# Inverses and scores as 64x64 tiles, and one plain key for two heads, in a gated delta-rule kernel

## The chip, the cores and the metric

One core of one Trainium2 chip runs the whole program. The metric is device time in microseconds (us) of one execution; the median of three runs stands for the kernel. Engines: PE (TensorE) multiplies matrices, PEld is its weight load, DVE (VectorE), ACT (ScalarE) and POOL (GpSimd) work on vectors, SP (SyncE) issues the DMAs. Each engine takes its instructions in the order in which the program lists them.

## The reference, cut to what matters

The input is 4 sequences of 1024 rows of 256 numbers. The attention has 16 key heads and 32 value heads of size 128 (two value heads share a key head), and works in chunks of 64 rows. For one value head and one chunk, with `k`, `q` normalized, `beta` the gate of the row, `gc` the running sum of the log decay:

```python
decay = exp(gc[i] - gc[j]) on and below the diagonal
A  = -(k_beta @ k.T * decay) * strictly_lower
Tm = inverse(eye - A)                         # 64 x 64: the "inverse"
u   = Tm @ v_beta
kcd = Tm @ (k_beta * exp(gc))
attn  = (q @ k.T) * decay                     # 64 x 64: the "scores"
v_new = u - kcd @ S                           # S: the state, 128 x 128
out   = (q * exp(gc)) @ S + attn @ v_new
S     = S * exp(gc[-1]) + (k * exp(gc[-1] - gc)).T @ v_new
```

The chunks of a sequence follow each other through `S`; sequences and heads do not depend on each other. The result is normalized, multiplied by `silu(z)` and projected; layer norms, residuals and a gated feed-forward layer follow, whose weights are looked up in a table of 16 numbers. All of it is in float32.

## The kernel before

The 32 value heads are handled in 8 groups of 4 (`HG`), with 2 key heads (`MG`) each. A step (`step`) handles one chunk of two sequences, `ab` = 0 and 1, for the 4 heads of a group: partitions 0 to 63 hold the 64 rows of one sequence, 64 to 127 those of the other. There are 256 steps. Eight steps make a `Super` (`SB`), of which there are 32. Two steps that follow each other belong to the two pairs of sequences, so that a state is used in every other step.

A step goes through six stages, separated by `yield`, and works as follows (lines are those of the profile):

- `pv`, `x0`: the values are transposed (L680) and scaled (L684).
- `pkqs`: key and query times state, two products in two banks (L693), one after the other. DVE adds the first to `x0` (L704, four instructions), ACT scales the second into `qs` (L705).
- `px`: inverse times `x0`, four matmuls of a full 128x128 array (L713), one a head. The weights `ue` hold the inverses of the two sequences as blocks on the diagonal, and zeros elsewhere. ACT copies `px` into `xs` (L718), negated.
- `pk`, `kt`: the keys are transposed (L722), and ACT makes four scaled copies, one for each head, by the factor `cd` of the row (L726). POOL decays the state (L730).
- `po`: scores times `xs`, four full matmuls (L713) with block-diagonal weights `ae`; DVE adds `qs` and makes `core` (L737). ACT squares `core` (L742).
- `pu`: key times `xs`, eight matmuls over 64 rows (L749); DVE adds the result to the state (L758).

`channel` makes the columns of q, k and v in advance (matmuls `pp` L432, a convolution over 4 rows: one ACT instruction L446 and three DVE instructions L449, silu L453). `norms` and `scores` make the squares, the factors `cc` (L505) and `cd` (L511) and the scores; `invert` finds 32x32 inverses on DVE (`rank` L589, `v` L590), and `build` completes them to 64x64 on PE (`m1`, `m2`). `expand` fetches the weights `ue`, `ae` and the chunk's key and query `qku` from DRAM for the step after. `project_out` makes `pz` (L143), transposes (`pto` L800) and projects (`pout` L807), and DVE adds the result to `ac` (L810 and L812).

The order is written out by hand: `SLOTS` gives one line for each of the eight steps of a super, in which each letter advances one generator by one stage. `N0`, `N1`, `N2` are the first three stages of the step, `O3`, `J`, `O4` the last three of the step before. A typical slot on PE is `pp` (A), `po` (O3), `pv` (N0), `pto` (T), `pu` (O4), `pkqs` twice (N1), `pz` (Z), `pp` (B), `px` and `pk` (N2), `pout` (U), with `kkq`, `pn` or `m1`, `m2` between in some slots.

All PSUM banks but those of `pp`, `pu` and `pgu` come from one pool of four (`bank`), handed out in turn: a bank is free once the readers of the bank that was handed out four allocations earlier are done. The doubles `pp` and `pu` come from a second pool of two.

Of the kernel before, what the change touches and what calls it, by code (L numbers as in the profile page):

```python
# [64 lines left out]
def delta_net_ffn_kernel(  # L65
# [128 lines left out]
    with tc.tile_pool(name="pre", bufs=2) as pre, tc.tile_pool(name="gates", bufs=1) as gp:  # L194
# [70 lines left out]
        for gs in range(0, NG, 4):  # L265
# [9 lines left out]
            for ab in range(2):  # L275
                ps = bank("pgate")
                T_.matmul(ps, lhsT=sel[ab], rhs=cols, start=True, stop=True)
                el = to[:, :, 4 * GW :].rearrange("p g (t a h) -> p a g t h", a=2, h=HG)[:, ab]
                A.activation(el, ps.rearrange("p (g t h) -> p g t h", g=4, h=HG), AF.Exp)
# [38 lines left out]
    with ExitStack() as main:  # L318
# [16 lines left out]
        zeroed = {}  # L335
        for name in ("ue", "ae"):
            zeroed[name] = [w1.tile(h4, F32, tag=f"{name}{i}", name=name) for i in range(NZ)]
            for t in zeroed[name]:
                G_.memset(t, 0.0)
# [5 lines left out]
        states = [w1.tile([P, 2, HG, P], F32, tag=f"S{p}", name="S") for p in range(NPAIR)]  # L345
# [4 lines left out]
        def load_qk(g):  # L350
# [9 lines left out]
            views.append(dk[:, 4 * nth :].rearrange("p (t a h) -> p t a h", a=2, h=HG))  # L360
# [38 lines left out]
        def channel(k, blk, n, far):  # L399

            last = k.last and blk == 1
            if n < 2 * MG:
                m, j = divmod(n, 2)
                if n == 0:
                    k.qk[blk] = [
                        w1.tile([P, 2, NPAIR, 2, 2, C], F32, tag=f"qk{i}", name=f"qk{i}", bufs=2)
                        for i in range(MG)
                    ]
                    if blk == 0:
                        k.qkd = sd.tile([SB, P, MG, 2, 2 * C], F32, tag="qkd", name="qkd")  # L410
                    if k.g not in w_qk:
                        load_qk(k.g)
                wt = w_qk[k.g][:, :, MG * j + m, :]
                ch = (NK if j else 0) + MG * k.g + m
                dst = k.qk[blk][m][:, :, :, 1 - j, :, :]
# [38 lines left out]
            if n < 2 * MG:  # L454
                nc.sync.dma_start(
                    k.qkd[4 * blk : 4 * blk + 4, :, m, 1 - j, :].rearrange("u p t -> p u t"),
                    dst.rearrange("p n q a t -> p (n q) (a t)"),
                )

        def norms(k, blk):  # L460

            if blk == 0:
                k.n2 = w2.tile([P, SB, MG, 2], F32, tag="n2", name="n2", bufs=5)
                k.cc = w2.tile([P, SB, HG], F32, tag="cc", name="cc", bufs=5)
                k.cd = w2.tile([P, SB, HG], F32, tag="cd", name="cd", bufs=5)
# [8 lines left out]
            for m in range(MG):  # L474
                for j in range(2):
                    src = k.qk[blk][m][:, :, :, j, :, :].rearrange("p n q a t -> p (n q) (a t)")
# [17 lines left out]
            for i in range(4):  # L494
# [16 lines left out]
            V.scalar_tensor_tensor(  # L511
                k.cd[:, us], k.cc[:, us], 1.0, dks[k.g][1][:, t0 : t0 + 4, :], ALU.mult, ALU.mult
            )

# [7 lines left out]
        def scores(k, blk):  # L522
# [24 lines left out]
            for n, (u0, dc) in enumerate(zip(us, dcs)):  # L547
# [3 lines left out]
                for p in range(2):  # L551
                    for m in range(MG):
                        src = k.qk[blk][m][:, n, p]
# [92 lines left out]
        def expand(k, u):  # L646

            at = (supers.index(k) * SB + u) % NZ
            ue, ae = (zeroed[name][at] for name in ("ue", "ae"))
            for q in range(4):  # L650
                rows = slice(q * BS, (q + 1) * BS)
                src = k.vd[q * BS + u * HG : q * BS + (u + 1) * HG, :, :]
                nc.sync.dma_start(ue[rows, :, rows], src.rearrange("h c i -> c h i"))
            for ab in range(2):
                a0 = ab * C
                lo, hi = slice(a0, a0 + BS), slice(a0 + BS, a0 + C)
                hb, w = divmod(u * HG, NQ)
                q = slice((2 * ab + hb) * BS, (2 * ab + hb + 1) * BS)
                nc.sync.dma_start(ue[lo, :, hi], k.nd[q, w : w + HG, :])
                half = slice(a0, a0 + C)  # L660
                nc.sync.dma_start(ae[half, :, half], k.atd[half, u, :, :])
            k.exp[u] = ue, ae
            qku = sc.tile([P, MG, 2, 2, C], F32, tag="qku", name="qku", bufs=2)
            nc.sync.dma_start(qku.rearrange("p m j a t -> p m j (a t)"), k.qkd[u])
            k.qku[u] = qku

        def step(k, u):
# [18 lines left out]
            if not first:  # L686
                got = []
                for j in range(2):
                    ps = bank("pkqs")
                    for m in range(MG):  # L690
                        two = slice(2 * m, 2 * m + 2)
                        for ab in range(2):
                            T_.matmul(  # L693
                                as4(ps)[ab * C : (ab + 1) * C, two, :],
                                lhsT=qk[:, m, j, ab, :],
                                rhs=S_[:, ab, two, :],
# [13 lines left out]
            def applied(w, src, name):  # L710
                ps = bank(name)
                for h in range(HG):
                    T_.matmul(as4(ps)[:, h, :], lhsT=w[:, h, :], rhs=src[:, h, :], start=True, stop=True)  # L713
                return ps

            px = applied(ue, x0, "px")
            xs = t4("xs")
            A.activation(xs, as4(px), AF.Copy, scale=-1.0)  # L718
            if not last:
                pk = bank("pk")  # L720
                for m in range(MG):
                    T_.transpose(as4(pk)[:, m, :], qk[:, m, 0].rearrange("p a t -> p (a t)"), ident)  # L722

                kt = t4("kt")
                for h in range(HG):
                    A.activation(kt[:, h, :], as4(pk)[:, h // 2, :], AF.Copy, scale=k.cd[:, u, h : h + 1])  # L726
                if not first:
                    flat = S_.rearrange("p a h d -> p (a h) d")
                    decay = el[:, ti].rearrange("p a h -> p (a h)").unsqueeze(2)
                    G_.tensor_tensor(flat, flat, bc(decay, [P, 2 * HG, P]), ALU.mult)  # L730
            yield
            po = applied(ae, xs, "po")
            core = t4("core", OUT_LAG)
            if first:
                V.tensor_copy(core, as4(po))
            else:
                V.tensor_tensor(core, as4(po), qs, ALU.add)  # L737
# [6 lines left out]
            if not last:  # L744
                pu = two_banks("pu")
                for h in range(HG):
                    for ab in range(2):
                        half = slice(ab * C, (ab + 1) * C)
                        T_.matmul(  # L749
                            as4(pu[:, ab])[:, h, :], lhsT=kt[half, h, :], rhs=xs[half, h, :], start=True, stop=True  # L750
# [418 lines left out]
```

## Time and profile before

| | |
|---|---|
| median of 3 runs | 4308.6 us (4305.1 to 4310.99) |
| span of the profiled execution | 4307.5 us; no other time of that execution is listed |
| busy PE / PEld / DVE / ACT / POOL | 3986.6 / 2899.0 / 3568.0 / 2831.6 / 2084.0 us |
| instructions | 83434 |
| steps of the delta rule | from about 250 to 3990 us of the span |
| DMA queue | 1052720 packets, 487.64 MB, 42.8% of 16 engines' span |
| granted TensorE clock | 0.984 in the mean, 1.00 from 1000 to 4000 us |

"Busy" is the time in which at least one instruction of the engine ran. A float32 matmul leaves two records, so `x2048` at L713 are 1024 matmuls. "Mean ns" of a matmul holds the time that its results take to come out, which overlaps with the next matmul; what a matmul costs is read from where the next one starts. A line `X <- Y` says that X sat idle until Y ended.

### The profile page before, as it was taken

To read this page: it belongs to the slowest core of one execution; us is meant where nothing else is said; L and a number is where in the kernel's file an instruction comes from. 1 tells how busy PE (TensorE), PEld (TensorE's weight loads), DVE (VectorE), ACT (ScalarE), POOL (GpSimd) and SP (SyncE) were. 2 spreads that over 40 slices of the span, in tenths; PEclk is the share of its full clock that TensorE was granted. 3 is DMA by queue.
4 is the path that set the end of the run, shared out by engine and by line. 5 is a ranking of instruction groups with operands and counts; after the bars stand their busy time and mean duration, and the time that the engine had idled before them with its cause. 6 is when DMAs were issued, how large, how long until landed. Compare 5 with 4: busy or idle time off the path is not lost.

```text
span 4307.5 us, 83434 instructions
## 1 busy us (share of the span) xinstructions
PE 3986.6 (93%) x28544; PEld 2899.0 (67%) x28544; DVE 3568.0 (83%) x6387; ACT 2831.6 (66%) x7279; POOL 2084.0 (48%) x1782
## 2 busy tenths in 40 slices
PE   3679999999999999999999999999999999999999
PEld 2457777777777777767777767777677777767454
DVE  4788888888999888888889998888888998886243
ACT  2467777776777767777677777777777777766211
POOL 2545555555555554555455554555454343434122
PEclk7899999999999999999999999999999999999999
DMA  3444444444444454544454445544454444543011
GB/s 94 120 112 113 116 121 116 123 122 119 128 131 116 114 135 129 134 115 115 129 137 122 109 116 138 135 120 114 121 139 124 119 115 124 137 108 102 26 41 28
DMA packets 1053140, 492.97 MB, mean 114 GB/s; under 512 B 730528, under 2 KB 951856, under 8 KB 1052720
## 3 DMA queue, kind: packets, MB, share of 16 engines
q1 hardware_dynamic: 1052720, 487.64, 42.8%
q8 instruction: 231, 3.78, 0.4%
q14 instruction: 189, 1.55, 0.1%
HBM read 267.66 MB, written 219.69 MB: 113 GB/s over the span
## 4 chain that ended last, share of the span: by engine, by line
PE 49%; DVE 36%; ACT 6%; issue 6%; DMA 2%; SPq 1%; POOL 0%; DVEq 0%; POOLq 0%; ACTq 0%
DVE cv L449 12%; PE pp L432 11%; DVE rank L589 7%; PE pkqs L693 6%; PE pz L143 6%; PE pout L807 5%; PE pgu L970 4%; PE po L713 3%; DVE v L590 3%; PE px L713 3%; DVE core L737 2%; PE pu L749 2%; PE kkq L555 2%; PE py L986 2%; DVE x L704 2%
## 5 line engine op out<-in xcount | busy, mean ns | idle before, releaser
L449 DVE SCALAR_TENSOR_TENSOR cv<-pp,cw,cv 128x512 f32<-128x512 f32 x1536 | 1148.7, 748 | 327.4 <-ACT cv L446 291.8
L794 POOL TENSOR_TENSOR zs<-zs,rr 128x512 f32<-128x512 f32 x256 | 267.4, 1045 | 1594.6 <-ACT zs L792 1584.6
L590 DVE TENSOR_TENSOR v<-v,rank 128x31 f32<-128x31 f32 (+15 forms) x992 | 624.1, 629 | 34.2 <-DVE rank L589 0.2
L589 DVE TENSOR_TENSOR rank<-v,lb 128x31 f32<-128x31 f32 (+15 forms) x992 | 578.3, 583 | 47.2 <-DMA lb<-ltd 41.8
L446 ACT ACTIVATE cv<-pp,cw 128x512 f32<-128x512 f32 x512 | 351.0, 686 | 375.5 <-PE pp L432 375.0
L432 PE MATMUL pp<-xnT,wq 128*128 128x262 f32 x2048 | 533.5, 403 | 50.1 <-DVE cv L449 36.2
L693 PE MATMUL pkqs<-S,qku 128*64 128x256 f32 x3840 | 493.4, 392 | 79.0 <-DVE core L737 50.4
L432 PEld LDWEIGHTS pp<-xnT,wq 128*128 128x128 f32 x2048 | 373.3, 192 | 223.7 <-issue 63.7
L432 PE MATMUL pp<-xnT,wv 128*128 128x262 f32 x2048 | 503.4, 387 | 6.3 <-DVE rank L589 4.0
L143 PE MATMUL pz<-wzs,xnT 128*64 128x512 f32 x2048 | 488.5, 598 | 5.1 <-DVE ac L812 4.3
L807 PE MATMUL pout<-wo,oT 128*128 128x256 f32 x2048 | 487.2, 381 | 1.5 <-ACT oT L802 0.7
L730 POOL TENSOR_TENSOR S<-S,dkm 128x1024 f32<-128x1024 f32 x224 | 435.0, 1942 | 21.6 <-PE pkqs L693 21.6
L742 ACT ACTIVATE junk<-core 128x128 f32<-128x128 f32 x1024 | 318.4, 311 | 172.9 <-DVE core L737 147.0
L432 PEld LDWEIGHTS pp<-xnT,wv 128*128 128x128 f32 x2048 | 380.8, 190 | 74.1 <-issue 12.2
L693 PEld LDWEIGHTS pkqs<-S,qku 128*64 128x64 f32 x3840 | 244.2, 137 | 250.9 <-DVE core L737 104.5
L807 PEld LDWEIGHTS pout<-wo,oT 128*128 128x128 f32 x2048 | 369.2, 190 | 49.8 <-ACT zs L792 4.4
L749 PE MATMUL pu<-xs,kt 64*128 64x128 f32 x3840 | 278.9, 285 | 65.2 <-DVE cv L449 65.2
L796 POOL TENSOR_TENSOR zs<-zs,core 128x512 f32<-128x512 f32 x256 | 326.5, 1275 | 20.0
L713 PEld LDWEIGHTS px<-x,ue 128*128 128x128 f32 x2048 | 263.3, 192 | 80.3 <-issue 32.5
L749 PEld LDWEIGHTS pu<-xs,kt 64*128 64x128 f32 x3840 | 233.1, 187 | 109.7 <-DVE cv L449 73.5
L310 POOL TENSOR_SCALAR lt<-lx,lutb 128x344 f32<-128x344 int32 (+2 forms) x210 | 279.4, 1331 | 16.8
L453 ACT ACTIVATE qk<-cv 128x512 f32<-128x512 f32 x256 | 162.0, 633 | 188.1 <-DVE cv L449 187.4
(185 smaller groups left out, 7208.1 us busy)
## 6 DMA issues: line engine op xcount, KB each, us to landing
qkd<-qk SPq DMA_DIRECT2D x256, 256.0 KB, 2.5
qku<-qkd SPq DMA_DIRECT2D x256, 256.0 KB, 2.9
dc<-rows_d SPq DMA_DIRECT2D x256, 128.0 KB, 3.3
ltd<-lT SPq DMA_DIRECT2D x128, 256.0 KB, 2.5
atd<-aT SPq DMA_DIRECT2D x128, 256.0 KB, 2.9
ae<-atd SPq DMA_DIRECT2D x512, 64.0 KB, 2.6
acc_d<-ac SPq DMA_DIRECT2D x256, 128.0 KB, 1.7
ac<-acc_d SPq DMA_DIRECT2D x224, 128.0 KB, 2.6
```

The costliest lines, as they stand in the source:

```text
L143: T_.matmul(ps[ab * C : (ab + 1) * C, :], lhsT=xnT[:, kc, 2 * p + ab, H + n * C : H + (n + 1) * C], rhs=rhs(kc), start=kc == 0, stop=kc == ...
L432: T_.matmul(ps[:, 2 * p : 2 * p + 2, : H + BT], lhsT=wt[:, kc, :], rhs=xnT[:, kc, 2 * p : 2 * p + 2, c0 : c0 + H + BT], start=kc == 0, sto ...
L446: A.activation(cv, ps[:, :, H : H + BT], AF.Copy, scale=cw[:, ch, H : H + 1])
L449: V.scalar_tensor_tensor(cv, ps[:, :, i : i + BT], cw[:, ch, i : i + 1], cv, ALU.mult, ALU.add)
L589: V.tensor_tensor(t, bc(v[:, 0 : j + 1, j : j + 1], sh), bc(lb[:, j : j + 1, j + 1 :], sh), ALU.mult)
L590: V.tensor_tensor(v[:, 0 : j + 1, j + 1 :], v[:, 0 : j + 1, j + 1 :], t, ALU.subtract)
L693: T_.matmul(as4(ps)[ab * C : (ab + 1) * C, two, :], lhsT=qk[:, m, j, ab, :], rhs=S_[:, ab, two, :], start=True, stop=True,)
L713: T_.matmul(as4(ps)[:, h, :], lhsT=w[:, h, :], rhs=src[:, h, :], start=True, stop=True)
L730: G_.tensor_tensor(flat, flat, bc(decay, [P, 2 * HG, P]), ALU.mult)
L749: T_.matmul(as4(pu[:, ab])[:, h, :], lhsT=kt[half, h, :], rhs=xs[half, h, :], start=True, stop=True)
L796: G_.tensor_tensor(zs, zs, k.cores.pop(u), ALU.mult)
L807: T_.matmul(pp[:, :HID], lhsT=oT[:, h, :], rhs=wo[:, h, :], start=h == 0, stop=h == HG - 1)
```

## The change

The blocks on the diagonal become tiles of their own: weights of 64 rows and 64 columns, eight matmuls for `px` and eight for `po`, whose four tiles (two row halves, two column halves) follow each other in the order of the program. The row half is the sequence `ab` in `px` and the key head `m` in `po`; a row half has a bank of its own, so `px` and `po` take two banks each. The transposed key goes into free columns of the `px` banks, before `px`, and no longer has a bank. It is copied once for a sequence, negated, with no factor; the factor `cd` goes onto a second, scaled copy of `px`, `xd`. With one key for two heads, `pu` has four matmuls of 256 columns where it had eight of 128. Layouts in SBUF and DRAM follow: `qk`, `qkd`, `qku`, `ue`, `ae`, the state, the decay of the state, and `cd`, which four small DMAs for each call of `norms` bring to the new partitions.

```diff
-                        w1.tile([P, 2, NPAIR, 2, 2, C], F32, tag=f"qk{i}", name=f"qk{i}", bufs=2)
+                        w1.tile([P, 2, 2, NPAIR, 2, C], F32, tag=f"qk{i}", name=f"qk{i}", bufs=2)
...
-                    k.qkd[4 * blk : 4 * blk + 4, :, m, 1 - j, :].rearrange("u p t -> p u t"),
-                    dst.rearrange("p n q a t -> p (n q) (a t)"),
+                    k.qkd[:, 1 - j, 4 * blk : 4 * blk + 4, :, m, :].rearrange("p u a t -> p (u a) t"),
+                    dst.rearrange("p n q a t -> p (n q a) t"),
...
-            V.scalar_tensor_tensor(
-                k.cd[:, us], k.cc[:, us], 1.0, dks[k.g][1][:, t0 : t0 + 4, :], ALU.mult, ALU.mult
-            )
+            cd = w2.tile([P, MG, 4, 2], F32, tag="cdt", name="cdt")
+            V.tensor_tensor(
+                cd.rearrange("p m u h -> p u m h"),
+                k.cc[:, us].rearrange("p u (m h) -> p u m h", h=2),
+                dks[k.g][1][:, t0 : t0 + 4, :].rearrange("p u (m h) -> p u m h", h=2),
+                ALU.mult,
+            )
+            for m in range(MG):
+                for ab in range(2):
+                    nc.sync.dma_start(k.cd[m * C : (m + 1) * C, blk, ab], cd[ab * C : (ab + 1) * C, m])
...
-            px = applied(ue, x0, "px")
-            xs = t4("xs")
-            A.activation(xs, as4(px), AF.Copy, scale=-1.0)
+            pxs = [bank("px") for _ in range(2)]
             if not last:
-                pk = bank("pk")
+                for ab in range(2):
+                    T_.transpose(pxs[ab][:, 2 * P : 3 * P], qk[:, 0, ab].rearrange("p m t -> p (m t)"), ident)
+            for n in range(2):
                 for m in range(MG):
-                    T_.transpose(as4(pk)[:, m, :], qk[:, m, 0].rearrange("p a t -> p (a t)"), ident)
-
-                kt = t4("kt")
-                for h in range(HG):
-                    A.activation(kt[:, h, :], as4(pk)[:, h // 2, :], AF.Copy, scale=k.cd[:, u, h : h + 1])
+                    for ab in range(2):
+                        T_.matmul(
+                            pxs[ab][m * C : (m + 1) * C, n * P : (n + 1) * P],
+                            lhsT=ue[ab * C : (ab + 1) * C, 2 * m + n, :],
+                            rhs=x0[ab * C : (ab + 1) * C, 2 * m + n, :],
+                            start=True,
+                            stop=True,
+                        )
+            xs = sc.tile([P, 2, 2, P], F32, tag="xs", name="xs")
+            for ab in range(2):
+                A.activation(xs[:, ab], pxs[ab][:, : 2 * P].rearrange("p (h d) -> p h d", h=2), AF.Copy, scale=-1.0)
+            if not last:
+                kt = sc.tile([P, 2, P], F32, tag="kt", name="kt")
+                xd = sc.tile([P, 2, 2, P], F32, tag="xd", name="xd")
+                for ab in range(2):
+                    A.activation(kt[:, ab], pxs[ab][:, 2 * P : 3 * P], AF.Copy, scale=-1.0)
+                    for n in range(2):
+                        A.activation(
+                            xd[:, ab, n, :],
+                            pxs[ab][:, n * P : (n + 1) * P],
+                            AF.Copy,
+                            scale=k.cd[:, blk, ab, un, n : n + 1],
+                        )
...
-            po = applied(ae, xs, "po")
+            pos = [bank("po") for _ in range(MG)]
+            for n in range(2):
+                for m in range(MG):
+                    for ab in range(2):
+                        T_.matmul(
+                            pos[m][ab * C : (ab + 1) * C, n * P : (n + 1) * P],
+                            lhsT=ae[m * C : (m + 1) * C, ab, n, :],
+                            rhs=xs[m * C : (m + 1) * C, ab, n, :],
+                            start=True,
+                            stop=True,
+                        )
             core = t4("core", OUT_LAG)
-            if first:
-                V.tensor_copy(core, as4(po))
-            else:
-                V.tensor_tensor(core, as4(po), qs, ALU.add)
+            for m in range(MG):
+                two = slice(2 * m, 2 * m + 2)
+                po = pos[m][:, : 2 * P].rearrange("p (h d) -> p h d", h=2)
+                if first:
+                    V.tensor_copy(core[:, two], po)
+                else:
+                    V.tensor_tensor(core[:, two], po, qs[:, two], ALU.add)
...
-                for h in range(HG):
-                    for ab in range(2):
-                        half = slice(ab * C, (ab + 1) * C)
+                for ab in range(2):
+                    for m in range(MG):
+                        half = slice(m * C, (m + 1) * C)
                         T_.matmul(
-                            as4(pu[:, ab])[:, h, :], lhsT=kt[half, h, :], rhs=xs[half, h, :], start=True, stop=True
+                            as4(pu[:, m])[:, 2 * ab : 2 * ab + 2, :],
+                            lhsT=kt[half, ab, :],
+                            rhs=xd[half, ab],
+                            start=True,
+                            stop=True,
                         )
```

In the prelude, the decay of the state is written by 16 ACT instructions of 128 columns where there were 4 of 512. The zeroed tiles of `ae` are gone, so three memsets on POOL go.

## The prediction

> **What bounds the kernel now.** I read the page first, for the engines and the chain that ended last.
>
> ```profile
> span 4307.5 us, 83434 instructions
> PE 3986.6 (93%) x28544; PEld 2899.0 (67%) x28544; DVE 3568.0 (83%) x6387; ACT 2831.6 (66%) x7279; POOL 2084.0 (48%) x1782
> ...
> PE 49%; DVE 36%; ACT 6%; issue 6%; DMA 2%; SPq 1%; POOL 0%; DVEq 0%; POOLq 0%; ACTq 0%
> ```
>
> PE looks like the bound, but the chain spends only half of its time on PE and a third on DVE: the two take turns. The span is 1.1 us under the median of 4308.6, so I work on the span and add the sum to the median. Next I read the busy time by stretch over the steps, 350 to 4000 us.
>
> ```profile
> 350.00:4000.00 3650.00, 3470.43 (x26135) 2590.59 (x26134) 3232.77 (x5684) 2610.00 (x6844) 1867.30 (x1538) 1.00 0.46 122
> ```
>
> There PE is busy for 95% of the time, DVE for 89%, ACT for 72%, the DMAs for 46%. 250 steps in 3650 us are 14.6 us a step, 117 us for a super of eight steps. PE can't gain more than some 10% before DVE stops it. The chain of waits over one super (2190 to 2312 us) shows the turns: DVE and ACT from 2190 to 2219, PE to 2248, DVE and ACT to 2279, PE to 2293, DVE again. So PE sets the time in 43 of these 122 us, three steps of eight, and in each super DVE hands over to PE twice. One hand-over, word for word from that chain:
>
> ```profile
> 2218.81 0.42 DVE ac L812
> ...
> 2219.27 1.08 PE pkqs L693 x8
> ...
> 2220.39 1.08 PE pkqs L693 x8
> ```
>
> What PE waits for in front of `pkqs` is named by the view of that tile:
>
> ```profile
>   DVE core L737: 154.9, 194
>   DVE ac L812: 55.6, 89
> ```
>
> Both are waits for a PSUM bank. Banks go round in turn, four in all. Before the change the order is `po pv pto pkqs pkqs pz px pk pout`, with a `kkq` or `pn` in between, so the first `pkqs` takes the bank of `pout`, which `ac` reads, and the second takes that of `po`, which `core` reads.
>
> **What a matmul costs.** The timeline of PE gives it by the starts.
>
> ```profile
> 2008.00 1.08 PE L621 MATMUL m<-pad,mt 128*32 128x128 f32 x32
> 2009.01 2.04 PE L432 MATMUL pp<-xnT,wv 128*128 128x262 f32 x8
> 2010.97 1.08 PE L635 MATMUL m<-pad,m 128*32 128x128 f32 x32
> ...
> 2024.97 1.93 PE L432 MATMUL pp<-xnT,wv 128*128 128x262 f32 x8
> 2026.74 1.05 PE L713 MATMUL po<-xs,ae 128*128 128x128 f32 x8
> 2027.63 0.60 PE L680 MATMUL pv<-ident,vt 128*128 128x128 f32 x4
> 2028.07 0.60 PE L800 MATMUL pto<-ident,zs 128*128 128x128 f32 x4
> 2028.60 1.16 PE L749 MATMUL pu<-xs,kt 64*128 64x128 f32 x16
> 2029.69 0.65 PE L693 MATMUL pkqs<-S,qku 128*64 128x256 f32 x4
> ```
>
> `po` to `pv` is 0.89 us for 8 records: 0.11 each, one tile of the full array. `pv` to `pto` is 0.44 for 4, the same. `pto` to `pu` is 0.53, so 0.09 more: here the shape of the tile changes. `pu` to `pkqs` is 1.09 for 16 records; two row halves at a time make 8 x 0.11 = 0.89, and 0.20 is left: 0.09 for the next change of shape and 0.11 for first weights of 128 columns, which nothing covers. `m` to `pp` is 1.01: 32 records, four column tiles at a time, make 0.88, and 0.13 is 0.09 for the change and some 0.04 for the first weights of 32 columns and the stagger. And `pp` between two changes takes 1.96 where it takes 1.77 without: 0.09 + 0.10. So a change of shape costs 0.09 us, and after it first weights cost 0.03 (32 columns) to 0.11 (128); for 64 I take 0.05.
>
> **The change, part by part (us a step).**
>
> `px`: before, `px` to `pk` is 0.89 and `pk` to `pout` 0.22. After, `pk` 0.22, a change 0.09, first weights 0.05, then 16 records with four tiles at a time, 4 x 0.11 = 0.44, stagger 0.02, a change 0.09, first weights of `pout` 0.11: 1.02 for 1.11, -0.09. `po`: 0.89 becomes 0.09 + 0.05 + 0.44 + 0.02 + 0.09 + 0.11 = 0.80, -0.09. `pu`: four matmuls of 256 columns are 4 rounds of 0.216 (`pkqs`, 8 rounds in 1.78 from 2015.04 to 2016.82), so 0.86 + 0.20 = 1.06 for 1.09, -0.03. Sum -0.2 on PE. No row shows 64x64 tiles. The nearest are `m` (four column tiles at once) and `pu` (two row halves at once), and I take four at once. The other bound is two at once: 8 rounds, 0.44 more for each product, +0.7 a step. The good bound, no cost for the changes of shape, is -0.9.
>
> The Trainium skill speaks for and against here. TensorEngine Tiling (Array Packing), Theoretical Speedup, gives up to 2x for each dimension that is 64 or less; eight matmuls four at a time would halve both products, by my estimate -0.9 a step or -225 us if all of it counted. Its section Key Properties says that a new tiling mode, as against a new tile of the same mode, drains the array first; it gives no time, and the rows above show 0.09 us and the uncovered weights. With both, -0.2 is left of -0.9.
>
> ACT: `xs` in two halves of 256 columns, `kt` two instead of four, and four `xd`. The rows that price it:
>
> ```profile
> L726 ACT ACTIVATE kt<-pk,cd 128x128 f32<-128x128 f32 x960 | 275.2, 383 | 0.0
> L737 DVE TENSOR_TENSOR core<-po,qs 128x512 f32<-128x512 f32 x240 | 163.8, 682 | 29.2 <-PE po L713 28.6 <-PE pv L680 0.5
> L812 DVE TENSOR_TENSOR ac<-ac,pout 128x256 f32<-128x256 f32 x224 | 91.8, 410 | 47.4 <-PE pout L807 46.7 <-DMA pad<-wgu_d 0.7
> ```
>
> A 128x128 instruction takes 275.2/960 = 0.29, a 256-column one (`x` from `pv`, 213.7 us for 512) 0.42; `xs` goes from 0.61 to 0.84. That is +0.23 + 2 x 0.29 = +0.8, some 195 us over 240 steps. I count it at nothing: from the end of `px` to `pv`, which now needs these banks, PE has `pout`, `pp` and `po`, over 4 us, and ACT needs 2.6. Without that cover it would be up to +0.8 a step.
>
> DVE: `core` is two instructions of 256 columns, like `ac`: 2 x 0.41 - 0.68 = +0.14, on the chain in about half of the steps: +0.55 a super. `cd` becomes the operation of `cc` (461 ns in the mean, 793 before; 0.97 against 0.5 where the chain passes them): twice a super, -0.8. Together -0.25 a super.
>
> SP and DMA: 256 more DMAs, four behind each `cd`, at 0.3 to 0.6 us of issue each; the loads for the next step stand behind them, but SP already waits at the store of `ac` for DVE (352.9 us for `rank` in SP's waits), and those loads are needed a step later. `qkd` has twice as many pieces of half the size, `ae` half as many; at 46% of the DMAs' time I count nothing. If it were not hidden, the loads would be late by about 2 us twice a super. The prelude gets 12 more small ACT instructions, 1 or 2 us.
>
> **The wait that is added.** The allocations are now `po po pv pto pkqs pkqs pz px px pout`. Four back from the first `pkqs` is the first `po`, from the second the second `po`; four back from `pto` is `pout` in five of eight slots. So `pto` waits for `ac`, with `pu` and both `pkqs` queued behind it on PE, and no `pkqs` starts before half of `core` is done. At the hand-over above, `ac` ended at 2219.23 and the second `pkqs` began at 2220.39. After: `pto` at 2219.26, `pu` 0.53 later, `pkqs` 1.06 later at 2220.85, the second 0.91 later (4 x 0.216 and 0.05) at 2221.76: +1.4. The other hand-over of this super:
>
> ```profile
> 2275.96 0.60 PE L800 MATMUL pto<-ident,zs 128*128 128x128 f32 x4
> 2277.75 1.16 PE L749 MATMUL pu<-xs,kt 64*128 64x128 f32 x16 [1.19 <-DVE cv L449]
> 2279.52 3.74 PE L693 MATMUL pkqs<-S,qku 128*64 128x256 f32 x16 [0.61 <-DVE ac L812]
> ```
>
> By the timeline of DVE, `ac` ended at 2279.47 and `core` ran from 2280.56 to 2281.24. After: `pto` 2279.5, `pu` 2280.03, `pkqs` 2281.09 and 2282.0, against 2281.3 for the second one before: +0.7. Together +2.1 a super, on the chain because PE leads it from there.
>
> **Sum.** PE -0.2 x 3 steps = -0.6, DVE -0.25, hand-overs +2.1: +1.25 a super, +40 us over 32. For what I set to nothing on ACT, SP and in the prelude I add 5: 4308.6 + 45 = 4354. Low bound of this case: half of the hand-over cost, +10 us. High bound: the new waits bite in every slot in which `ac` or `core` ends late. In five or six slots the same reckoning gives 0.3 to 1.4, some 5 a super; less 1.6 for PE that is +3.5, +110 us, 4420.
>
> **Rivals.**
> 1. *Faster*: the hand-overs cost nothing, because DVE, relieved of `cd` and met by a later PE, has `ac` done before `pto`. Then -0.6 - 0.25 a super gives -27 us, 4282; with all of PE's -0.2 x 256 it is 4257. For it: in three slots of eight `pto` does not take `pout`'s bank. Against it: the waits for `core`, 154.9 us at 194 places. It decides if a hand-over costs under 0.4.
> 2. *Four tiles don't run at once.* Two at once: 0.9 us more a step than I count; on three steps of a super that is +2.7, +85 us: 4440. The page's `pu` and `m` rows speak against it.
> 3. *No change*: the terms cancel, 4300 to 4317.
>
> **How the numbers follow.** Forecast (slower by the bank waits) 0.58, own range 4318 to 4420; rival 1 0.26; rival 2 0.09; rival 3 0.07. What a measurement of this kernel can tell from no change is about 0.2%, 9 us. Faster 0.26, same 0.07, slower 0.67. The range goes from 4270, which holds most of rival 1, to 4430, the top of the forecast; beyond lie rival 2 and the far end of rival 1.
>
> **What would show it.** In the profile after: `px` and `po` 64*64 with 16 records in about 0.5 us from first to last start; 0.09 us more at each change; PE waits in front of `pto` for `ac` and in front of the first `pkqs` for `core`, more than 155 + 56 us together; PE's busy time lower by 30 to 60 us and its share down; ACT busy about 190 us more. If those waits do not grow, the forecast is wrong; if `px` needs 0.9 us, rival 2 is right.

## The result, and the profile after

The changed kernel takes 4488.69 us (4483.1 to 4491.05, four runs) where the kernel before takes 4308.31 (4305.1 to 4310.99, four runs): the ratio is 1.0415, with a 95% interval of 1.04 to 1.043. It is 180 us slower. The forecast was slower by 45, its range ended at 4430, and the result lies outside.

The page of the kernel after:

```profile
span 4489.3 us, 90020 instructions
PE 3995.8 (89%) x30720; PEld 2623.8 (58%) x30720; DVE 3636.8 (81%) x6643; ACT 2940.7 (66%) x8027; POOL 2083.7 (46%) x1779
...
PE 41%; DVE 41%; issue 7%; ACT 5%; DMA 3%; SPq 2%; POOL 1%; DVEq 0%; POOLq 0%; ACTq 0%
```

Every engine's share of busy time is lower than before or the same, in a longer span. PE's busy time hardly moved, 3995.8 against 3986.6 us, and its place in the chain fell from 49 to 41%. The stretch of the steps (length, then busy time and instructions of PE, PEld, DVE, ACT, POOL, then the granted TensorE clock, the DMA share and GB/s) has the number that matters most:

```profile
350.00:4000.00 3650.00, 3325.41 (x26908) 2226.36 (x26910) 3161.97 (x5637) 2595.34 (x7176) 1789.17 (x1465) 0.96 0.46 117
```

The last column but two is 0.96, and was 1.00 before: the clock that PE was granted fell in the steps. The mean over the whole span went from 0.984 to 0.957. The share of the DMAs is the same 0.46.

The waits of PE, with the total in us, how often, and the longest:

```profile
PE pto L838 <- DVE ac L850: 184.8, 104, 3.8
PE pkqs L703 <- DVE core L771: 68.8, 54, 2.4
```

Before, `pto` had no wait for `ac`, and PE's own waits in front of `pkqs` were these (in the prediction, 154.9 and 55.6 us hold the waits of the weight load, PEld, as well):

```profile
PE pkqs L693 <- DVE core L737: 50.4, 52, 2.4
PE pkqs L693 <- DVE ac L812: 23.5, 44, 0.9
```

The place at which the two meet, on PE's timeline in the second slot of a super (start, duration, line, operation, number of records, and in brackets the idle time before it):

```profile
2317.50 0.67 PE L757 MATMUL po<-xs,ae 64*64 64x128 f32 x16
2318.10 0.66 PE L690 MATMUL pv<-ident,vt 128*128 128x128 f32 x4
2321.71 1.09 PE L838 MATMUL pto<-ident,zs 128*128 128x128 f32 x4 [2.95 <-DVE ac L850]
2322.72 2.08 PE L783 MATMUL pu<-xd,kt 64*128 64x256 f32 x8
2324.73 3.32 PE L703 MATMUL pkqs<-S,qku 128*64 128x256 f32 x16
...
2332.76 0.67 PE L727 MATMUL px<-x,ue 64*64 64x128 f32 x16
2333.36 0.92 PE L845 MATMUL pout<-wo,oT 128*128 128x256 f32 x3
```

And the same stretch by its busy times, cut at the wait and at the end of `pkqs`:

```profile
2310.00:2318.00 8.00, 8.00 (x64) 5.63 (x60) 7.72 (x15) 6.80 (x20) 4.17 (x3) 1.00 0.52 143
2318.00:2321.70 3.70, 0.76 (x12) 0.44 (x5) 3.60 (x7) 3.66 (x5) 1.84 (x2) 0.87 0.00 0
2321.70:2327.90 6.20, 6.19 (x30) 3.75 (x32) 5.14 (x14) 4.35 (x14) 2.42 (x3) 0.53 0.42 108
2327.90:2334.00 6.10, 6.10 (x55) 4.06 (x52) 4.40 (x6) 2.95 (x8) 3.37 (x3) 1.00 0.00 0
```

Read the two together. PE runs out of work at 2318.8 and stands idle until `ac` ends at 2321.56. In the 6.2 us that follow it is busy all the time, but at a clock of 0.53 in the mean: `pto` to `pu` takes 1.01 us (0.53 in the kernel before), `pu` to `pkqs` 2.01 (1.06 is what the forecast worked out), `pkqs` 3.16 (1.78). These are the matmuls that the others wait for. DVE gets `pkqs` late, stands idle for 0.92 us in front of `x` and for 1.67 before the scores. At 2327.6 the clock is whole again.

The trace has the granted clock and every idle stretch of PE, so that this can be counted over the steps. Before, no idle stretch was longer than 2.35 us, and PE ran at half clock for 13.7 us in four stretches. After, there are 50 idle stretches of over 2.5 us (40 of over 3, the longest 3.84), all in front of `pto`, and 279.9 us at half clock in 49 stretches. They come up to twice a super, in slots 2 and 6 of the eight. In the mean of the 28 supers in the middle of the run, a super got 6.1 us longer (118.8 to 124.9 us), of which these two slots have 5.5.

When the clock falls can be read from the same records. In each run, every half-clock stretch starts a whole number of times 3.413 us after any other, to within 0.01 us. Cut into pieces of this length, the place above reads:

```profile
2317.32:2320.73 3.41, 1.44 (x22) 0.84 (x20) 3.27 (x7) 3.33 (x7) 0.87 (x1) 1.00 0.03 5
2320.73:2324.14 3.41, 2.43 (x10) 1.91 (x12) 3.34 (x8) 3.40 (x8) 3.23 (x4) 0.50 0.20 64
2324.14:2327.56 3.42, 3.42 (x18) 1.69 (x16) 2.43 (x7) 1.91 (x9) 0.16 (x1) 0.50 0.56 133
```

PE is busy for 1.44 us of the first piece, less than half, and the clock is at half in the next one. In the steps of the kernel after, all 49 falls come behind a piece in which PE was busy for at most 49%; the 990 pieces at whole clock behind which it stayed whole have 50% or more. Before, the four falls come behind 39 to 47%, and the clock stayed whole behind 48% or more. In some of the runs below the border is less sharp (a few falls behind pieces of up to 57%, and some pieces of down to 41% without one). So what counts is PE's idle time in such a piece, in one stretch or in several, and not the length of one stretch.

PE's own work got shorter, as the forecast had it. With each group of matmuls taken at its shortest distance to the next, so without waits and at the whole clock, PE's work is an estimated 109 us a super, and was 111; the difference is a little over 2 us.

### The profile page after: what moved, and what is told of

Its sections match the earlier page's. It is cut to its first block, busy times and chain, and to the rows that moved or that the text cites. A ratio compares the mean times of both kernels' runs of the same rounds, so it can differ in the third digit from the quotient of the medians.

```text
span 4489.3 us, 90020 instructions
## 1 busy us (share of the span) xinstructions
PE 3995.8 (89%) x30720; PEld 2623.8 (58%) x30720; DVE 3636.8 (81%) x6643; ACT 2940.7 (66%) x8027; POOL 2083.7 (46%) x1779
## 3 DMA queue, kind: packets, MB, share of 16 engines
q14 instruction: 204, 1.67, 0.1%
## 4 chain that ended last, share of the span: by engine, by line
PE 41%; DVE 41%; issue 7%; ACT 5%; DMA 3%; SPq 2%; POOL 1%; DVEq 0%; POOLq 0%; ACTq 0%
DVE cv L452 12%; PE pp L435 8%; DVE rank L599 8%; PE pkqs L703 6%; DVE v L600 5%; PE pz L143 5%; PE pu L783 4%; PE pgu L1008 4%; PE pout L845 4%; DVE S L796 3%; DVE x L714 3%; PE pto L838 2%; PE py L1024 2%; DVE ac L850 1%; DVE rr L803 1%
## 5 line engine op out<-in xcount | busy, mean ns | idle before, releaser
L600 DVE TENSOR_TENSOR v<-v,rank 128x31 f32<-128x31 f32 (+15 forms) x992 | 637.0, 642 | 34.0
L599 DVE TENSOR_TENSOR rank<-v,lb 128x31 f32<-128x31 f32 (+15 forms) x992 | 607.5, 612 | 69.0 <-DMA lb<-ltd 63.6
L703 PE MATMUL pkqs<-S,qku 128*64 128x256 f32 x3840 | 516.7, 416 | 69.4 <-DVE core L771 68.8
L845 PE MATMUL pout<-wo,oT 128*128 128x256 f32 x2048 | 510.3, 392 | 3.7 <-ACT nT L494 2.8
L703 PEld LDWEIGHTS pkqs<-S,qku 128*64 128x64 f32 x3840 | 276.6, 149 | 296.1 <-DVE core L771 111.8
L838 PE MATMUL pto<-ident,zs 128*128 128x128 f32 x1024 | 177.4, 301 | 219.7 <-DVE ac L850 184.8
L715 ACT ACTIVATE qs<-pkqs,dkm 128x128 f32<-128x128 f32 x960 | 270.9, 363 | 86.7 <-PE pkqs L703 86.7
L783 PE MATMUL pu<-xd,kt 64*128 64x256 f32 x1920 | 316.5, 454 | 5.5 <-DVE cv L452 5.3
L743 ACT ACTIVATE xd<-px,cd 128x128 f32<-128x128 f32 x960 | 316.0, 406 | 0.0
L714 DVE SCALAR_TENSOR_TENSOR x<-pkqs,dkm,x 128x128 f32<-128x128 f32 x960 | 269.1, 343 | 43.9 <-PE pkqs L703 42.9
```

Of the source, the lines that this page charges most:

```text
L599: V.tensor_tensor(t, bc(v[:, 0 : j + 1, j : j + 1], sh), bc(lb[:, j : j + 1, j + 1 :], sh), ALU.mult)
L600: V.tensor_tensor(v[:, 0 : j + 1, j + 1 :], v[:, 0 : j + 1, j + 1 :], t, ALU.subtract)
L703: T_.matmul(as4(ps)[ab * C : (ab + 1) * C, two, :], lhsT=qk[:, j, ab, m, :], rhs=S_[:, m, ab], start=True, stop=True,)
L714: V.scalar_tensor_tensor(x0[:, h, :], as4(got[0])[:, h, :], e, x0[:, h, :], ALU.mult, ALU.add)
L783: T_.matmul(as4(pu[:, m])[:, 2 * ab : 2 * ab + 2, :], lhsT=kt[half, ab, :], rhs=xd[half, ab], start=True, stop=True,)
L845: T_.matmul(pp[:, :HID], lhsT=oT[:, h, :], rhs=wo[:, h, :], start=h == 0, stop=h == HG - 1)
```

## The experiments

The theory: two banks for `po` make `pto` wait for `ac`; the wait leaves PE idle for about 3 us; the clock then falls, and this costs more than the wait. The rivals: the copies of `px` on ACT; the smaller instructions on DVE; the new layouts and DMAs; the bank wait by itself, with the clock only a sign of it. Each comparison is with the kernel before on the same chip, whose medians were 4306.3 to 4311.2 us. Where two of the runs are set against each other, the chips can differ, and by these medians that is worth up to 5 us.

### One bank for `po`, the rest of the change kept

The scores' weights are padded with zeros to full rows, so that the key head needs no row half and `po` goes into one bank again; `core` is one instruction.

```diff
-            pos = [bank("po") for _ in range(MG)]
+            po = bank("po")
...
-                            pos[m][ab * C : (ab + 1) * C, n * P : (n + 1) * P],
-                            lhsT=ae[m * C : (m + 1) * C, ab, n, :],
-                            rhs=xs[m * C : (m + 1) * C, ab, n, :],
+                            as4(po)[ab * C : (ab + 1) * C, 2 * m + n, :],
+                            lhsT=ae[:, m, ab, n, :],
+                            rhs=xs[:, ab, n, :],
```

> The changed kernel, but the scores go back to 128 rows, padded with zeros, in tiles of 128x64, so that po needs one bank and core is one instruction again. PE gets 0.4 us a step more than in the changed kernel; the order of the banks is that of before, px px in place of px pk. Theory (the bank turn makes PE wait for ac): the waits of the transposes for ac go, no idle stretch of PE is over 2.5 us, clock 1.00, 4300 to 4360. Rival 1 (tiles of 64 rows, DMA layout, cd on SP, or the additional ACT work are the cost): 4490 or more, since PE has more to do.

Measured: 4333.77 us, ratio 1.005 (1.0035 to 1.0065). By the same estimate as above PE has some 3 us a super more to do than in the changed kernel, and the whole is 155 us faster. No idle stretch of PE in the steps is over 2 us, and the half clock is back at 13.7 us. PE's waits in it:

```profile
PE pu L783 <- DVE cv L455: 48.3, 54, 2.0
PE pkqs L706 <- DVE core L771: 45.8, 55, 1.6
```

The wait of `pto` for `ac` is gone. What follows: all but some 23 of the 180 us hang on the second bank of `po` and on `core` in halves, which the next two runs part. The other layouts, the DMAs of `cd`, the tiles of `px` and the copies on ACT are all still in this run, and with them it is 23 us above the kernel before.

### Two banks for `po`, the rest of the change left out

The kernel before, with full matmuls, but the product in two banks and `core` in two halves.

```diff
-            po = applied(ae, xs, "po")
+            pos = [bank("po") for _ in range(MG)]
+            for h in range(HG):
+                T_.matmul(as4(pos[h // 2])[:, h % 2, :], lhsT=ae[:, h, :], rhs=xs[:, h, :], start=True, stop=True)
```

> The kernel before, with full matmuls and everything as it was, but po spread over two banks and core in two halves: the bank turn of the changed kernel alone. Theory (bank turn, then clock): as slow as the changed kernel or slower, 4460 to 4540, clock about 0.96 over the steps, the transposes waiting for ac. Rival 1 (tiles, layouts, ACT work): 4308 to 4345, the price of core in two halves.

Measured: 4441.13 us, 1.0303 (1.0286 to 1.0321), the clock in the mean 0.971, 143.4 us at half clock, 51 idle stretches of over 2.5 us. Its first two waits of PE:

```profile
PE pto L805 <- DVE ac L817: 155.0, 104, 3.3
PE pkqs L693 <- DVE core L742: 56.6, 56, 2.4
```

Neither a 64x64 tile nor a second copy of `px` is in it, and the same wait, as often as in the changed kernel (104 times), with half as much time at half clock, costs 130 us. That is a little less than the 4460 us and more that the theory expected, and far from the rival's 4345.

### `core` in two halves, one bank

```diff
+            for m in range(MG):
+                two = slice(2 * m, 2 * m + 2)
+                po = as4(pq)[:, two]
...
+                    V.tensor_tensor(core[:, two], po, qs[:, two], ALU.add)
```

> The kernel before with core in two instructions of 256 columns, banks as they were: the price of that part alone. +0.14 us on DVE in 240 steps, on the chain in about half of them: 4315 to 4345 by every theory; if it were over 4400, the halved core and not the bank turn would explain the run with two po banks.

Measured: 4328.32 us, 1.0044 (1.0029 to 1.0059), that is +19 us. With the 130 of the run before, the bank turn without the split of `core` costs about 111, if the two simply add up.

### More work for PE in the idle time

The changed kernel; in slots 2 and 6 the transposes of `pv` are made three times (and, in another run, five times), each time into the same place.

```diff
-            for h in range(HG):
-                T_.transpose(as4(pv)[:, h, :], vt[h][:, un * P : (un + 1) * P], ident)
+            for _ in range(3 if u in (1, 5) else 1):
+                for h in range(HG):
+                    T_.transpose(as4(pv)[:, h, :], vt[h][:, un * P : (un + 1) * P], ident)
```

> The changed kernel, with the four transposes of the values (pv) issued three times over in two of eight steps (u = 1 and 5, the two slots in which the transposes of zs wait some 3 us for ac). It only adds work to PE: 2 x 0.9 us a super, 64 x 0.9 = 56 us in all, in the shade of that wait. Theory (the wait itself is cheap, but an idle stretch of over 3 us on PE makes the granted clock fall to half for the next 3.4 to 6.8 us): the stretches of idle PE shrink to some 2.2 us, the clock stays at 1.00 over the steps, and the time falls by 90 to 170 us, to 4320 to 4400. Rival 1 (the bank wait costs by its place in the chain, the clock is a side show): same time, 4480 to 4500. Rival 2 (DMA, ACT or DVE work): same time or up to 50 us slower.

> The changed kernel, with the transposes of the values issued five times over in the two slots of a super where it had three times over in the run before. The wait for ac is filled but for some 1.2 us. Theory (clock falls with idle PE): clock 1.00 over all steps, and what is left is the price of the bank turn without the clock: 4340 to 4390. Rival (the filling itself delays PE): above 4408.

Measured: three times, 4408.5 us, 1.0223 (1.0195 to 1.0251), 68.3 us at half clock; five times, 4394.57 us, 1.0193 (1.0176 to 1.021), 34.1 us at half clock. Both are a little slower than the theory expected (4400 and 4390 at most), and with three the clock did not stay whole. The kernel with five, by its stretch of the steps and its first wait of PE:

```profile
350.00:3950.00 3600.00, 3370.60 (x28168) 2305.13 (x28168) 3206.21 (x5727) 2614.41 (x7270) 1811.00 (x1485) 1.00 0.47 120
```

```profile
PE pto L839 <- DVE ac L851: 105.5, 96, 2.1
```

The wait for `ac` is still there, 96 times; only the idle time in front of it is shorter, since PE transposes the same values again and again. The clock is at 1.00, and the kernel is 94 us faster than the change, though it only has more to do. That is what the clock costs, and a lower bound of it: the filling costs something too. The next run shows what.

> The kernel before with the transposes of the values three times over in the same two slots: the control of the filling. Its clock is 1.00 already and its idle stretches there are 1.1 us, so 0.9 us of added work is hidden in part: both theories 4309 to 4350, and no gain.

Three transposes for one in the kernel before: 4321.49 us, 1.0028 (1.0017 to 1.0038), +12 us. So adding work costs time where PE was not idle for long, and saves time where it was.

### Without the scaled copies of `px`

The run with one bank for `po`, without the four `xd`; `pu` uses `xs`, and the key is scaled by a constant. It leaves out the decay factor of the row in the state, so it prices the copies and computes something else. (The copies were also left out of the run with `pout` beside `po`, below, with no constant; its values did not stay finite, and there is no time.)

```diff
-                    for n in range(2):
-                        A.activation(
-                            xd[:, ab, n, :],
-                            pxs[ab][:, n * P : (n + 1) * P],
-                            AF.Copy,
-                            scale=k.cd[:, blk, ab, un, n : n + 1],
-                        )
...
-                            rhs=xd[half, ab],
+                            rhs=xs[half, ab],
```

> As the run with po in one bank (whose clock is steady), without the four scaled copies xd of each step; pu multiplies by xs, and the key is scaled by a constant instead, so the factor of the decay is left out of the state. ACT has 1.15 us a step less to do than in that run and less than before the change. It prices ACT's added work where no bank turn is in the way. Theory (ACT's copies lie in the shade of pout, pp and po): 4320 to 4340, within 12 us of that run's 4334. Rival (ACT's work is a part of the loss): 4310 or less.

Measured: 4294.39 us, 0.9963 (0.9949 to 0.9977). The engines on its page:

```profile
PE 4003.3 (93%) x30720; PEld 2674.3 (62%) x30720; DVE 3551.6 (83%) x6387; ACT 2681.9 (62%) x7067; POOL 2080.8 (48%) x1782
```

The four copies cost 39 us (4333.77 to 4294.39), though ACT is busy for 68% of the span with them and 62% without: they are not hidden, as I had counted them in the prediction and once more in the expectation, whose rival (4310 or less) holds. Without them, and with one bank, the 64x64 tiles and the plain key are 0.4% faster than the kernel before, by less work than the reference asks for.

### Attempts to keep the tiles and avoid the wait

Four runs tried other orders of the banks, and one another engine for `xd`.

`pv` in the free halves of the two `po` banks, so that the turn has one bank less:

```diff
-            pv = bank("pv")
+            pvs = [bank("po") for _ in range(MG)]
+            halves.append(pvs)
...
-            pos = [bank("po") for _ in range(MG)]
+            pos = halves.pop() if halves else [bank("po") for _ in range(MG)]
```

> All of the change (64x64 tiles, one plain key, layouts, additional ACT work, cd on SP), but the transposed values of the next step go into the free halves of the two banks of po, issued ahead of po. A step then takes nine allocations again, and the first pkqs waits for ac, the second for half of core, as before the change; the transposes of zs wait for ACT alone. Theory (bank turn, and the clock that falls with it, are the whole loss): no idle stretch of PE over 2.5 us, clock 1.00 over the steps, 4270 to 4330: PE's work is 2.3 us a super less than before the change, core in halves costs DVE 1.1 us. Rival (a part of the loss is the additional ACT work, the layouts or SP): clock 1.00, but 4350 or more.

Measured: 4398.82 us, 1.0205 (1.019 to 1.0221), 58 us at half clock. The wait has another place: ACT's `x` waits for DVE's `core` (412.7 us at 208 places) and `pkqs` for `x` (124.0 us at 155), so the two readers of a shared bank now follow each other. The expectation (4270 to 4330) failed, and as a test of the bank turn the run says nothing. It has only 3 idle stretches of over 2.5 us in its steps; 14 of its 16 falls of the clock come behind pieces in which no idle stretch is over 2 us. The same with the matmul `po` ahead of `x0` and `core` behind it:

> As the run with shared banks, where ACT's reading of the transposed values had come to wait for core; now the scores are multiplied ahead of that reading and core stands behind it, so that ACT waits for PE alone and core waits for ACT. All of the change otherwise. Theory: the first pkqs waits for ac, the second for half of core; no idle stretch of PE over 2.5 us but where ACT is late with its exponentials (two slots of eight, core up to 1 us later): 4300 to 4370. Rival (any further wait on a bank costs as much): about 4400.

Measured: 4420.4 us, 1.0252 (1.0233 to 1.0271), 71.7 us at half clock; `pz` now waits for `core` (120.4 us at 132 places). This expectation failed too.

`pout` in the free half of the next step's first `po` bank, with `ac` added just ahead of `core`:

```diff
-            pos = [bank("po") for _ in range(MG)]
+            pos = [halves.pop() if halves else bank("po"), bank("po")]
...
-            pp = bank("pout")
+            free = bank("po")
+            halves.append(free)
+            pp = free[:, 2 * P :]
```

> All of the change, but pout takes the free half of the first bank of po of the step that follows, and DVE adds it to ac just ahead of core. Nine allocations a step: the transposes of zs wait for ACT (px) and no longer for ac; the first pkqs waits for ac and the first half of core, the second for the second half. Theory (the bank turn in front of the transposes, and the clock that falls with it, are the loss): no idle stretch of PE over 2.5 us, clock 1.00 over the steps, 4270 to 4350. Rival (ACT's added work, layouts, SP): clock 1.00 but 4370 or more.

Measured: 4434.47 us, 1.0285 (1.0268 to 1.0302), 187.7 us at half clock. `pto` has no wait for `ac` any more, but the kernel is only 54 us faster than the change and not at the 4270 to 4350 that were expected, for PE now stands in front of the first `pkqs`:

```profile
PE pkqs L704 <- issue: 207.7, 133, 2.8
```

Of its 42 idle stretches of over 2.5 us, 40 are there, and the longest is 2.82. The clock falls here too, whichever matmul waits, and less than 3 us is enough.

Two rings of banks, one for the short-lived tiles and three for the rest, and `pto` behind `pu`:

```diff
+        if name in QUICK:
+            return psum.tile([P, 512], F32, tag="pq", name=name, bufs=1)
+        return psum.tile([P, 512], F32, tag="ps", name=name, bufs=3)
...
-            "A v1 O3 N0 v1 T J O4 N1 Z s v1 B N2 n v1 U",
+            "A v1 O3 N0 v1 J O4 T N1 Z s v1 B N2 n v1 U",
```

> The changed kernel with the four banks dealt out in two turns: one bank for pv, pto, kkq, pn, m1 and m2, three for the others, and the transposes of zs one place later (behind pu). The first pkqs then waits for ac, the second for the first half of core, as before the change. Theory: clock 1.00, PE's waits in front of the transposes gone, 4260 to 4340, by the PE work saved and the halved core. Rival 1 (tiles, layouts, ACT work): about 4490. Rival 2 (a single bank for six uses makes new waits): waits for ACT in front of pto or kkq, 4350 to 4450.

Measured: 4560.59 us, 1.058 (1.0564 to 1.0596), the slowest of all, where 4260 to 4340 were expected. It has only 9 idle stretches of over 2.5 us, but 303.8 us at half clock. Its trace shows that one long gap is not needed: around 1085 us, for one, PE is idle for 1.6 us in front of `pu`, works about 1 us, and is idle for 2.1 us in front of `pto`, whose wait is the first in its list:

```profile
PE pto L841 <- POOL lt L318: 100.8, 49, 3.5
```

Last, one bank for `po` and `xd` as one instruction of POOL in place of four of ACT:

```diff
+                G_.tensor_tensor(xd, xs, bc(k.cd[:, blk, :, un, :].unsqueeze(3), [P, 2, 2, P]), ALU.mult)
```

> The attempt at a version that beats both: po in one bank, and the second copy xd made by one POOL instruction of 512 columns from xs, with the factor, in place of four on ACT; the key is copied without the sign. All of the reference is computed. If ACT's four copies are what is left (the run without them gave 4294), 4294 to 4312; if the POOL instruction (about 1.05 us a step, behind the decay of the state in POOL's order or ahead of it) holds up the pu product or DVE, 4315 to 4350.

Measured: 4367.36 us, 1.0141 (1.0124 to 1.0158), 116 us at half clock. Its waits of PE in front of `pu`:

```profile
PE pu L777 <- DVE cv L455: 109.1, 58, 2.6
...
PEld pu L777 <- POOL dc L559: 60.2, 35, 2.2
```

That is beyond the 4315 to 4350 expected for the case that POOL holds up `pu`. The instruction takes 1.04 us and stands behind `dc` and others in POOL's queue; all 22 idle stretches of over 2.5 us are in front of `pu`. Why the wait for `cv` grew as well, no run shows. No version that computes the whole reference was faster than the kernel before.

## Why the prediction was right or wrong, step by step

**PE's products: right.** `po` to `pv` and `px` to `pout` are 0.60 us on the timeline above, first weights and change of shape included; the 16 records start within 0.40 us, so four tiles run at once. The forecast had 0.71 in the same way of counting, and -0.2 us a step; the estimate by the super, a little over 2 us in eight steps, is nearly -0.3. Rival 2 (two tiles at a time) is out.

**The added wait: the right place, the wrong size.** `pto` waits for `ac`, PE has `pu` and `pkqs` behind it, and this is what makes the kernel slower. Rival 1, that `ac` would be done in time, is out, and rival 3 with it. The step that failed is the pricing of the hand-over: +1.4 and +0.7 us were worked out with `pto`, `pu` and `pkqs` at the full-speed durations of the trace before. After a wait of 3 us they do not run at full speed. This term, not in the sum at all, is worth at least the 94 us that filling the idle time brought.

The trace of before had shown the price, at the very hand-over that the prediction quotes. The two rows, of the first and of the second hand-over:

```profile
2219.27 2.21 PE L693 MATMUL pkqs<-S,qku 128*64 128x256 f32 x16 [0.46 <-DVE ac L812]
2279.52 3.74 PE L693 MATMUL pkqs<-S,qku 128*64 128x256 f32 x16 [0.61 <-DVE ac L812]
```

The same 16 records take 2.21 us in the one and 3.74 in the other, and the busy times of the two pieces around 2279.73 show why:

```profile
2276.32:2279.73 3.41, 1.61 (x21) 1.17 (x21) 3.34 (x6) 3.38 (x6) 3.25 (x4) 1.00 0.00 0
2279.73:2283.14 3.41, 3.41 (x18) 1.57 (x16) 3.30 (x6) 2.35 (x10) 0.67 (x1) 0.50 0.25 63
```

PE had been idle for 1.19 and 0.61 us, and then ran at half clock. (The second half of this `pkqs` waits for `core`, which ends at 2281.24, so not all of the difference is lost time.) It happened four times in the steps of before, so the stretch from 350 to 4000 us still shows 1.00.

The idle time could have been worked out from the same rows, too. At the first hand-over of the forecast, `pv` ended in the kernel before at 2215.94, where `pto` followed it at once; `pu` then waited 1.11 us for `cv`, and `pkqs` 0.46 for `ac`. With `pto` held until 2219.26 nothing stands in between: the two short waits and the work between them become one idle stretch of some 3.3 us. At the second hand-over it is about 3.5 us, from 2275.96 to 2279.5. The forecast counted by how much the ends move and never asked how long PE would stand still.

The Trainium skill, TensorE: Matmul & The Clock Gate, Part 1: The HAM clock gate, says that PE's clock is halved after an idle window of about 3.4 us and restored after a busy one, and in the section Why this matters for your kernels it advises to keep idle gaps under some 3 us. The direction agrees with the runs; the size of the gap does not quite: 40 gaps of at most 2.82 us brought the clock to half as well in the run with `pout` beside `po`, and one of 2.35 us, or 1.19 and 0.61 us close together, did in the kernel before.

**ACT's copies: counted at nothing, and wrong.** By groups ACT got about what was forecast: `xd` 316.0 and `kt` 144.8 us for `kt` 275.2, and `xs` 170.5 for 155.2, together +201 us against 195. (The page's busy time rose only by 109, as ACT's instructions overlap each other.) But the cover that I named does not hold: the run without `xd` took 243 us of ACT's busy time away (2924.5 to 2681.9) and gained 39 us. For the change's +109 of the same measure that makes an estimate of 39 x 109/243 = 17 us; by the groups, of which that run took 351 us away, it is 39 x 201/351 = 22.

**DVE: one half right, one half wrong.** From the groups by shape:

```profile
L771 DVE TENSOR_TENSOR core<-po,qs 128x256 f32<-128x256 f32 x480 | 179.8, 415 | 11.1 <-PE po L757 7.3 <-ACT cv L449 2.9 <-POOL zs L834 0.4
L515 DVE TENSOR_TENSOR cdt<-cc,dkm 128x16 f32<-128x16 f32 x64 | 49.2, 769 | 2.2
```

`core` costs 2 x 0.37 us a step for 0.68, and the run with halves alone gave +19 us where the sum had 0.55 x 32 = 18. The new `cd` was to cost as much as `cc`, 0.8 us a super less than the old one. It takes 769 ns in the mean, where the old one took 793, and the median of both is 966: the other operation is no cheaper here, and the -26 us have no ground. (From the prediction's own figures, twice 0.97 less 0.5, it would have been -0.9 a super.)

**The sum again.** Forecast +45, less the 5 set aside for ACT, SP and the prelude, plus 26 for `cd`, plus some 20 for ACT, plus 94 for the clock: +180, which is what was measured. The agreement is luck: the 94 is a lower bound, and the 20 is an estimate. What the bank turn costs at full clock was not measured by itself: the sum still holds the forecast's 67 us for it. The second bank cost 155 us in all; less 94 for the clock and 19 for `core`, 42 are left, to which comes what some 3 us a super more work on PE cost in the run with one bank. That lies about where the forecast had it, and no run settles it better.

**What would show it.** PE's waits in front of `pto` and `pkqs` grew as announced (184.8 us for `ac` where there were none, 68.8 for `core` where there were 50.4), and the products have the starts that were named. PE's busy time was to fall by 30 to 60 us and rose by 9: a matmul at half clock counts as busy for about twice as long, and this hid the gain on the page.

## What to carry to other kernels

When a change puts a wait in front of a matmul, work out how long PE will stand idle there, from the end of its last matmul to the end of what it waits for, and add the other idle stretches close by. If PE can be idle for more than half of some 3.4 us, price the following 3 to 7 us of matmuls at half speed. Look in the trace of before for a place where it has already happened, by the rows that take twice as long as others of their shape. A product that takes one more bank of a shared ring moves every reader that the ring waits for; go round the ring and name the new pairs before counting what the product itself saves. Read the granted clock by stretches beside PE's busy share: a share that stays high while the span grows can be a slow clock.

## What the runs showed of the hardware

- In the steps, the clock falls to half for 3.41 or 6.83 us, on a grid of 3.413 us, behind a piece of the grid in which PE was busy for less than about half (all 49 falls of the kernel after at 49% or less, none behind a piece at whole clock with 50% or more; over all runs the border lies between 41 and 57%). The idle time need not be in one stretch: 1.19 and 0.61 us were enough in the kernel before, and 1.6 and 2.1 us with 1 us of work between in the run with two rings. In the kernel after, most half-clock stretches follow each other at 61.4 or 64.9 us, 18 or 19 times 3.41.
- In the kernel after, the half clock went on for another 3.41 us behind a piece at half clock in which PE was busy for 39 to 87%, and ended behind 90% or more.
- Work that nobody needs can save time: a group of four transposes, 0.44 us, made twice more in two slots of eight, took 80 us off the changed kernel and put 12 on the kernel before.
- Eight 64x64 matmuls (16 records) start within 0.40 us, four at a time, the four tiles being two row halves and two column halves; with first weights and the change of shape the group takes 0.60 us.
- On DVE, 128x16 operands with a stride take from 0.17 to 0.97 us, with a median of 0.97 both as one operation with two tensors and as the operation with a scalar in between (0.77 and 0.79 in the mean). What makes some of them five times as long as others, no run shows.
